# One stored row per node for both of its experts, and two groups of rows in the buffer, in a graph layer followed by a mixture of experts

## The chip, the cores and the metric

The kernel runs on one NeuronCore of a Trainium2 chip. A core has five engines with a queue each, which run their instructions in order and wait for each other through semaphores: TensorE (PE in the profile; its weight loads are the row PEld), VectorE (DVE), ScalarE (ACT), GpSimd (POOL) and SyncE (SP). Transfers go through 16 DMA engines; SP and POOL issue nearly all of them here. The metric is device time in microseconds of one launch, median of several runs. Every launch computes the whole reference, in float32.

## The reference

There are 6250 nodes with 256 features and 100,000 edges with 96 features, sorted by the node that they point to. The first half is a graph layer, the second half a mixture of 16 experts, of which each node uses two:

```python
out1 = segment_sum(edge_attr, col);  out2 = segment_max(edge_attr, col)
out3 = out1 / max(count, 1)
h = concat([layernorm(x), out1, out2, out3, u[batch]], axis=1)
x = x + relu(h @ W1 + b1) @ W2 + b2 + layernorm(x)

n = layernorm(x)
vals, idx = top_k(n @ gate_w + gate_b, 2)
wts = softmax(vals)
moe = sum(wts[k] * (relu(n @ w1[idx[k]] + b1[idx[k]]) @ w2[idx[k]] + b2[idx[k]]) for k in 0, 1)
x = x + layernorm(n + moe) * gamma + beta
```

## The kernel before

**Nodes.** Nodes are cut into 50 columns of 125 and these into 13 groups, the first of two columns and the others of four, taken from the last node to the first. A list of tasks with slot numbers (12 slots for a group) is sorted by slot, and within a slot by the order of entry; each task then appends its instructions to the engines' queues. A slot has no time: it only says where in the queues an instruction stands. The scan over the edges (`steps`, lines 298 to 302, on VectorE) is woven in between by a credit of estimated costs, so that it runs up to about 790 us.

**A group's way.** For a group that starts at slot B, the hidden layer (line 747) and the output layer (line 755) of the graph layer take the slots from B on. Its edge sums are gathered from memory by GpSimd (`take_edges`, line 698, and `take_carry`, line 705) and joined on VectorE (line 711). From slot B + 13 on, the group is prepared for the experts: `norm_b` (line 783, ScalarE) normalises the rows into the buffer `xr`; `turn_b` (line 792) transposes them on TensorE; `logits`, `choose`, `rank`, `rank_2` and `place` find the two best experts of each node, the two weights, and the place of the row in the list of each of the two experts; `send` (line 860) writes the rows to `xg_d` in memory, by two indirect transfers of GpSimd for each column, one for each expert.

**The row.** A row of `xg_d` is 256 normalised features, one weight and one number that says where the result is to go (`DR` = 258 words). The two copies of a node differ in those two words, so `xr` holds both: `[P, GS, 2, DR]`, in a pool with one buffer. `norm_b` of the next group therefore waits until all transfers of the group before have read the buffer.

**Experts.** `table_full` and `table_rest` cut the expert lists into 57 blocks of 256 rows. `to_row` turns a table of expert numbers and offsets into a row, from which SP reads registers in `load_block`: the block's rows `xb`, 1 MB of expert weights `wt` and a bias `eb`. `run_block(b)` runs two layers on TensorE (lines 1034 and 1047). Between the two halves of the first layer it calls `turn_block(b + 1)`, so on VectorE the order within a block is: the copy of the next block's transposed rows (line 1014), the bias added to its rows (line 1017), the destination (line 1019, or lines 1022 and 1023 from block 14 on), and only then the two activations of this block's second half (line 1038). The second layer needs four hidden parts of 128: parts 0 and 2 come from ScalarE (line 1040), parts 1 and 3 from line 1038, and TensorE takes them in the order 0, 2, 1, 3. After line 1050, ScalarE multiplies the rows by their weight (line 1052) and GpSimd scatters them to `y_d` (line 1053).

**End.** A last loop adds the two results of each node, normalises, and writes the output (lines 1365 to 1389).

Of the kernel before, what the change touches and what calls it, by code (L numbers as in the profile page):

```python
# [9 lines left out]
F32 = mybir.dt.float32  # L10
# [4 lines left out]
OP = mybir.AluOpType  # L15
# [4 lines left out]
P = 125  # L20
# [21 lines left out]
def kernel(  # L42
# [34 lines left out]
    B1O = W2O + FC * D  # L77
    WROW = B1O + FC
    NB = (2 * N - NE) // SB + NE
    DR = D + 2  # L80
    NG = (NT + GS - 1) // GS
    ER = EP * sum(JR)

# [16 lines left out]
    def halves(o, i):  # L100
# [14 lines left out]
    nc.gpsimd.memset(ones, 1.0)  # L115
    node_i = const.tile([P, NT], F32, name="node_i")
    nc.gpsimd.iota(node_i, pattern=[[P, NT]], base=0, channel_multiplier=1,
                   allow_small_or_imprecise_dtypes=True)
    place_i = const.tile([P, NT, 2], F32, name="place_i")
    nc.gpsimd.iota(place_i, pattern=[[P, NT], [N, 2]], base=0, channel_multiplier=1,  # L120
                   allow_small_or_imprecise_dtypes=True)
    erow = const.tile([P, NE], F32, name="erow")
    nc.gpsimd.iota(erow, pattern=[[N, NE]], base=0, channel_multiplier=0, allow_small_or_imprecise_dtypes=True)
# [64 lines left out]
    gtp = mlp.enter_context(tc.tile_pool(name="gt", bufs=2))  # L188
    sm = mlp.enter_context(tc.tile_pool(name="sm", bufs=2))
    xrp = mlp.enter_context(tc.tile_pool(name="xr", bufs=1))  # L190
    pTp = banks.enter_context(tc.tile_pool(name="pT", bufs=1, space=PSUM))
    accp = banks.enter_context(tc.tile_pool(name="acc", bufs=5, space=PSUM))
    pGp = banks.enter_context(tc.tile_pool(name="pG", bufs=1, space=PSUM))
# [583 lines left out]

    def norm_b(g):
        a, z = GRP[g]
        G[g]["xr"] = xr = xrp.tile([P, GS, 2, DR], F32, name="xr")  # L780
        for i in range(z - a):
            t = a + i
            nc.scalar.activation(xr[:, i, :, 0:D], G[g]["xt"][:, i, None, :].to_broadcast([P, 2, D]), AF.Identity,
                                 scale=stat[:, 0, t:t + 1], bias=stat[:, 1, t:t + 1])

    def turn_b(g, k):
        n = GRP[g][1] - GRP[g][0]
        if k == 0:
            G[g]["gT"] = gtp.tile([128, DC, GS * P], F32, name="gT", bufs=1)
        pT = pTp.tile([128, GS * P], F32, name="pT")  # L790
        for i in range(n):
            nc.tensor.transpose(pT[:, i * P:(i + 1) * P], G[g]["xr"][:, i, 0, k * 128:(k + 1) * 128], ident[:P, :P])
        nc.scalar.copy(G[g]["gT"][:, k, :n * P], pT[:, :n * P])

    def logits(g):
# [20 lines left out]
    def rank(g):  # L816
        a, z = GRP[g]
        n, m0 = z - a, NT - z
        i2 = gtp.tile([P, GS, 2], F32, name="i2")
        nc.vector.tensor_copy(i2[:, :n], G[g]["I8"][:, :n, 0:2])  # L820
        G[g]["mk"] = mk = gtp.tile([P, GS, 2, NE], F32, name="mk")
        nc.vector.tensor_tensor(mk[:, :n], i2[:, :n, :, None].to_broadcast([P, n, 2, NE]),
                                row_i[:P, None, None, 0:NE].to_broadcast([P, n, 2, NE]), op=OP.is_equal)
        mm = gtp.tile([P, GS, NE], F32, name="mm")
        nc.vector.tensor_add(mm[:, :n], mk[:, :n, 0], mk[:, :n, 1])
        for i in range(n):
            nc.vector.tensor_add(M[:, m0 + i + 1, :], M[:, m0 + i, :], mm[:, i, :])
        G[g]["mm"] = mm
# [9 lines left out]
    def place(g):  # L838
        a, z = GRP[g]
        n, xr, mk, dv = z - a, G[g]["xr"], G[g]["mk"], G[g]["dv"]  # L840

        rk = gtp.tile([P, GS, NE], F32, name="rk")
        nc.vector.tensor_tensor(rk[:, :n], G[g]["pR"][:, :n * NE].rearrange("p (i e) -> p i e", e=NE),
                                erow[:, None, :].to_broadcast([P, n, NE]), op=OP.add)
        nc.vector.tensor_tensor(mk[:, :n], mk[:, :n], rk[:, :n, None, :].to_broadcast([P, n, 2, NE]), op=OP.mult)
        posf = gtp.tile([P, GS, 2], F32, name="posf")
        nc.vector.tensor_reduce(posf[:, :n], mk[:, :n], AX.X, OP.add)
        G[g]["pos"] = pos = xrp.tile([P, GS, 2], I32, name="pos_i", bufs=2)
        nc.vector.tensor_copy(pos[:, :n], posf[:, :n])

        w0 = gtp.tile([P, GS], F32, name="w0")
        nc.vector.tensor_scalar(w0[:, :n], dv[:, :n], 1.0, None, op0=OP.add)
        nc.vector.reciprocal(w0[:, :n], w0[:, :n])
        nc.vector.tensor_copy(xr[:, :n, 0, D], w0[:, :n])
        nc.vector.tensor_mul(xr[:, :n, 1, D], w0[:, :n], dv[:, :n])
        nc.vector.tensor_copy(xr[:, :n, :, D + 1], place_i[:, a:z, :])  # L856

    def send(g, i):
        for k in range(2):
            d = nc.gpsimd.indirect_dma_start(out=xg_d[:, :],  # L860
                                             out_offset=IndirectOffsetOnAxis(ap=G[g]["pos"][:, i, k:k + 1], axis=0),
                                             in_=G[g]["xr"][:, i, k, :], in_offset=None)
            tc.declare_no_dep(d.ins, group="rows", reason="each row has a place of its own")
            tc.add_to_no_dep_group("rows", d.ins)
            nc.gpsimd.memset(gap, 0.0)
# [6 lines left out]
    def open_experts():  # L872
        edges_until(len(JR) - 1)
        assert next(stream, None) is None
        edges.close()
        MB["pools"] = pools = ExitStack()
        for nm, bufs in (("tb", 1), ("wp", 3), ("xg", 4), ("bk", 3)):
            MB[nm] = pools.enter_context(tc.tile_pool(name=nm, bufs=bufs, side="right"))
        tb = MB["tb"]
        MB["half"] = half = tb.tile([128, 2], F32, name="half_i")  # L880
        nc.gpsimd.iota(half, pattern=[[1, 2]], base=0, channel_multiplier=2, allow_small_or_imprecise_dtypes=True)
        MB["tab_a"] = tb.tile([1, 2, NA], I32, name="tab_a")
        MB["tab"] = tb.tile([1, 2, NB - NA], I32, name="tab")
        MB["seen"] = tb.tile([128, NB - NA], F32, name="seen")
        MB["more"] = tb.tile([1, 1], I32, name="more")
        for nm in ("cnt_e", "full", "nbf", "cum", "ge", "own"):
            MB[nm] = tb.tile([NB, NE], F32, name=nm)
        MB["nbi"] = tb.tile([NB, NE], I32, name="nbi")
        for nm in ("jc", "q", "skip"):
            MB[nm] = tb.tile([NB, 1], F32, name=nm)  # L890
        MB["er"] = tb.tile([NB, 2], F32, name="er")
# [33 lines left out]
        nc.vector.tensor_scalar(jc[:n], jc[:n], float(SB), None, op0=OP.mult)  # L925
        nc.vector.scalar_tensor_tensor(er[:n, 1:2], er[:n, 0:1], float(N), jc[:n], op0=OP.mult, op1=OP.add)

    def to_row(tab, n):
        pe = eps.tile([1, 2, n], F32, name="ps")
        for k in range(2):  # L930
            nc.tensor.matmul(pe[:, k, :], MB["er"][:n, k:k + 1], ident[:n, :n], start=True, stop=True)
        nc.vector.tensor_copy(tab, pe)

    def table_full_2():
        to_row(MB["tab_a"], NA)

    def table_rest():
        n = NB - NA
# [26 lines left out]

    def table_rest_2():
        n = NB - NA
        to_row(MB["tab"], n)
        ps = pGp.tile([128, n], F32, name="pg")
        nc.tensor.matmul(ps, MB["skip"][:n].to_broadcast([n, 128]), ident[:n, :n], start=True, stop=True)  # L970
        nc.vector.tensor_copy(MB["seen"], ps)
# [35 lines left out]
    def turn_block(b):  # L1007
# [7 lines left out]
        BL[b]["to"] = to_i = MB["xg"].tile([128, 2], I32, name="to_i")  # L1015

        nc.vector.tensor_tensor(xb[:, :, 0:D], xb[:, :, 0:D], BL[b]["eb"][:, None, :].to_broadcast([128, 2, D]), op=OP.add)
        if b < NA:
            nc.vector.tensor_copy(to_i, xb[:, :, D + 1])
        else:  # L1020
            far = MB["xg"].tile([128, 2], F32, name="far")
            nc.vector.tensor_scalar(far, MB["half"], MB["seen"][:, b - NA:b - NA + 1], float(2 * N), op0=OP.is_lt, op1=OP.mult)
            nc.vector.tensor_tensor(to_i, xb[:, :, D + 1], far, op=OP.add)

    def run_block(b, end):
        xT, wt, xb = (BL[b][nm] for nm in ("xT", "wt", "xb"))
# [22 lines left out]
        yb = MB["bk"].tile([128, 2, D], F32, name="yb")  # L1049
        nc.vector.tensor_tensor(yb, pY, xb[:, :, 0:D], op=OP.add)  # L1050
        for h in range(2):
            nc.scalar.activation(yb[:, h, :], yb[:, h, :], AF.Copy, scale=xb[:, h, D:D + 1])  # L1052
            d = nc.gpsimd.indirect_dma_start(out=y_d[:, :],  # L1053
                                             out_offset=IndirectOffsetOnAxis(ap=BL[b]["to"][:, h:h + 1], axis=0),
                                             in_=yb[:, h, :], in_offset=None, bounds_check=2 * N - 1, oob_is_err=False)
            tc.declare_no_dep(d.ins, group="back", reason="each row has a place of its own")
            tc.add_to_no_dep_group("back", d.ins)
            nc.gpsimd.memset(gap, 0.0)
# [29 lines left out]
    for g, (a, z) in enumerate(GRP):  # L1088
# [40 lines left out]
        at_slot(B + SLOTS + 9, rank_2, g)  # L1129
        at_slot(B + SLOTS + 10, place, g, cost=1.5)  # L1130
        for i in range(n):
            at_slot(B + SLOTS + 11 + i // 2, send, g, i)
    T = SLOTS * (NG - 3) + 21
    at_slot(T, open_experts)
    at_slot(T, count_full)
# [28 lines left out]

    def fill_rows():

        nc.vector.memset(fill[:, D + 1:], float(2 * N))
        for h in range(SB // 128):
            nc.gpsimd.dma_start(xg_d.rearrange("(e n) d -> n e d", n=N)[h * 128:(h + 1) * 128],
                                fill[:, None, :].to_broadcast([128, NE, DR]))  # L1170
# [37 lines left out]
    cut_x = windows_of(xrp.tile([P, GS, 2, DR], F32, name="xr"), 1)[0]  # L1208
# [229 lines left out]
```

## Time and profile before

| what | us |
|---|---|
| median of three runs | 1454.03 (1452.14 to 1459.58) |
| the profiled execution, its own time | 1462.48 |
| its span, first to last instruction | 1460.7 |
| TensorE busy (matmuls) | 1148.5 |
| VectorE busy | 915.6 |
| GpSimd busy | 527.8 |
| ScalarE busy | 511.0 |

In the profile, a row of a timeline gives the start in us, the duration, the engine, the line of the kernel, the operation, the tiles written and read with their shapes, and in brackets the idle time of the engine just before, with what ended it. A line of the waits gives the engine and its line, what it waited for, the total in us, the number of waits and the longest. A line of the windows gives the stretch, its length, then for each engine the busy time with the number of instructions, then the granted TensorE clock, the busy share of the DMA engines and GB/s.

The span has three parts. Up to about 905 us the graph layer and the routing run. From there to 1355 us the 57 expert blocks run, the first ten of them between the last pieces of the routing. The rest is the last loop.

### The profile page before, as it was taken

The numbers are of one execution on the slowest core, as the hardware profiler recorded it, in microseconds if no ns is written. First come the engines' busy times: TensorE is split into PE (matmuls) and PEld (weight loads), VectorE is DVE, ScalarE is ACT, GpSimd is POOL, SyncE is SP. The second block draws the span as 40 slices with busy tenths as digits, with TensorE's granted clock in tenths as the row PEclk, the third lists the DMA queues.
The fourth block names the chain that finished last, engine by engine and source line by source line (L and its number), as shares of the span: only waits on it lengthen the run. The fifth ranks groups of instructions, "written<-read, shape, count | busy, mean of one in ns | idle before, by whom it ended". The sixth has DMA issues, their size and how long they took to land.

```text
span 1460.7 us, 16116 instructions
## 1 busy us (share of the span) xinstructions
PE 1148.5 (79%) x4667; PEld 810.4 (55%) x4667; DVE 915.6 (63%) x2322; ACT 511.0 (35%) x1174; POOL 527.8 (36%) x611
## 2 busy tenths in 40 slices
PE   2857258978786879999688999899999999999200
PEld 1743144635443445655445567787888888888100
DVE  4487569959685979988688323244344544444397
ACT  3384125543445542542325441321212222212133
POOL 4133033563546553364242522234333333333100
PEclk9988579989988889999899999899999999999655
DMA  6726777787778897888887332646777787765695
GB/s 180 168 63 172 187 193 201 194 224 182 216 192 247 223 277 190 254 223 213 249 221 206 84 122 69 209 147 235 229 250 262 234 267 234 237 226 184 128 263 148
DMA packets 173812, 292.25 MB, mean 200 GB/s; under 512 B 30883, under 2 KB 119656, under 8 KB 166414
## 3 DMA queue, kind: packets, MB, share of 16 engines
q1 hardware_dynamic: 137374, 234.35, 56.0%
q0 software_dynamic: 36224, 56.33, 13.7%
q8 instruction: 40, 0.66, 0.2%
q14 instruction: 62, 0.51, 0.1%
q10 hardware_dynamic: 112, 0.41, 0.1%
HBM read 169.70 MB, written 123.21 MB: 201 GB/s over the span
## 4 chain that ended last, share of the span: by engine, by line
issue 27%; DVE 23%; DMA 18%; POOL 13%; PE 12%; ACT 3%; SPq 2%; POOLq 0%; DVEq 0%; ACTq 0%
POOL y_d L1053 9%; PE acc L747 5%; DMA raw<-in_edge_dram 5%; DMA cg<-carry_d,next_i 4%; DMA rows_d<-rw 3%; PE acc L755 3%; DVE rw L302 2%; DVE rw L299 2%; DVE rw L298 2%; DMA xg_d<-xr,pos_i 2%; DVE rw L301 2%; POOL gb L474 1%; PE acc L570 1%; DMA carry_d<-ct 1%; DVE o L1387 1%
## 5 line engine op out<-in xcount | busy, mean ns | idle before, releaser
L747 PE MATMUL acc<-inT,w1x 128*128 128x500 f32 (+1 forms) x832 | 375.9, 603 | 0.0
L747 PEld LDWEIGHTS acc<-inT,w1x 128*128 128x128 f32 x832 | 163.1, 204 | 179.1 <-issue 177.3
L1053 POOL DMA_INDIRECT y_d<-yb,to_i x114 | 134.5, 1180 | 295.6 <-ACT yb L1052 273.4
L1034 PE MATMUL acc<-xT,wt 128*128 128x256 f32 x912 | 225.6, 391 | 7.8 <-ACT hb L1040 6.2
L1047 PE MATMUL acc<-wt,hb 128*128 128x256 f32 x912 | 209.6, 383 | 3.6 <-DVE hb L1038 3.6
L860 POOL DMA_INDIRECT xg_d<-xr,pos_i x100 | 130.1, 1301 | 213.8 <-DVE xr L856 152.2
L755 PE MATMUL acc<-w2s,hT 128*125 128x256 f32 x800 | 193.5, 400 | 13.4 <-ACT hT L749 13.4
L1034 PEld LDWEIGHTS acc<-xT,wt 128*128 128x128 f32 x912 | 171.0, 193 | 40.2 <-ACT hb L1040 14.9
L1047 PEld LDWEIGHTS acc<-wt,hb 128*128 128x128 f32 x912 | 175.3, 192 | 29.0 <-DVE hb L1038 4.5
L755 PEld LDWEIGHTS acc<-w2s,hT 128*125 128x125 f32 x800 | 157.8, 201 | 39.5 <-ACT hT L749 14.2
L1052 ACT ACTIVATE yb<-yb,xb 128x256 f32<-128x256 f32 x114 | 51.8, 501 | 349.0 <-issue 291.6
L1050 DVE TENSOR_TENSOR yb<-acc,xb 128x512 f32<-128x512 f32 x57 | 39.4, 692 | 167.3 <-PE acc L1047 167.3
L749 ACT ACTIVATE hT<-acc,c 128x500 f32<-128x500 f32 (+1 forms) x104 | 68.5, 658 | 209.0 <-PE acc L747 209.0
L474 POOL DMA_INDIRECT gb<-in_dst_dram,blk_i x50 | 71.1, 1421 | 130.5 <-DVE blk_i L471 73.8
L301 DVE TENSOR_TENSOR rw<-rw,raw 125x768 f32<-125x768 f32 x88 | 83.6, 950 | 32.7 <-DMA raw<-in_edge_dram 32.7
L298 DVE TENSOR_TENSOR rw<-rw,keep 125x768 f32<-125x768 f32 x81 | 78.3, 966 | 34.0 <-DMA rows_d<-rw 23.7
L1014 DVE COPY xT<-pT 128x512 f32<-128x512 f32 x57 | 39.4, 690 | 72.4 <-PE pT L1012 71.5
L302 DVE TENSOR_TENSOR rw<-rw,raw 125x768 f32<-125x768 f32 x88 | 83.6, 950 | 0.0
L299 DVE TENSOR_TENSOR rw<-rw,bar 125x768 f32<-125x768 f32 x81 | 79.4, 981 | 0.0
L705 POOL DMA_INDIRECT cg<-carry_d,next_i x44 | 65.1, 1481 | 36.8 <-issue 23.6
L698 POOL DMA_INDIRECT at<-rows_d,first_i x44 | 60.0, 1363 | 37.2 <-PE acc L747 10.0
L732 ACT COPY inT<-pT 128x500 f32<-128x500 f32 (+1 forms) x65 | 36.0, 553 | 98.8 <-PE pT L731 94.8
(296 smaller groups left out, 1445.1 us busy)
## 6 DMA issues: line engine op xcount, KB each, us to landing
wt<-in_wpack_dram SPq DMA_DIRECT2D x57, 1026.0 KB
rows_d<-rw SPq DMA_DIRECT2D x27, 1440.0 KB
rows_d<-rw SPq DMA_DIRECT2D x27, 810.0 KB
raw<-in_edge_dram SPq DMA_DIRECT2D x27, 720.0 KB
xb<-xg_d SPq DMA_DIRECT2D x57, 258.0 KB
raw<-in_edge_dram SPq DMA_DIRECT2D x27, 405.0 KB
yk<-y_d SPq DMA_DIRECT2D x20, 400.0 KB
eb<-in_eb_dram SPq DMA_DIRECT2D x57, 128.0 KB
```

Source lines behind the costliest of these rows:

```text
L298: nc.vector.tensor_tensor(su, prev[0], keep[c][:, :, s + j, None].to_broadcast(bcast), op=OP.mult)
L299: nc.vector.tensor_tensor(mx, prev[1], bar[c][:, :, s + j, None].to_broadcast(bcast), op=OP.min)
L301: nc.vector.tensor_tensor(su, su, x_j, op=OP.add)
L302: nc.vector.tensor_tensor(mx, mx, x_j, op=OP.max)
L474: nc.gpsimd.indirect_dma_start(out=gbs_[t], out_offset=None, in_=dst_b, in_offset=IndirectOffsetOnAxis(ap=blk_i[:, t:t + 1], axis=0))
L747: nc.tensor.matmul(pH[:, :n * P], w1x[:, k, ms], inT[:, k, :n * P], start=False, stop=(k == KC - 1))
L749: nc.scalar.activation(h[:, :n * P], pH[:, :n * P], AF.Relu, bias=c1[:, m:m + 1])
L755: nc.tensor.matmul(pO, G[g]["hT"][m][:, i * P:(i + 1) * P], w2s[:, m, :], start=(m == 0), stop=(m == HC - 1))
L860: d = nc.gpsimd.indirect_dma_start(out=xg_d[:, :], out_offset=IndirectOffsetOnAxis(ap=G[g]["pos"][:, i, k:k + 1], axis=0), in_=G[g]["xr"][ ...
L1034: nc.tensor.matmul(pB[i][:, half, :], wt[:, k * FF + m * 128:k * FF + (m + 1) * 128], xT[:, k, :], start=(k == 0), stop=(k == DC - 1))
L1047: nc.tensor.matmul(pY[:, h, :], hb[:, m, h * 128:(h + 1) * 128], wt[:, W2O + m * D:W2O + (m + 1) * D], start=(m == order[0]), stop=(m == o ...
L1053: d = nc.gpsimd.indirect_dma_start(out=y_d[:, :], out_offset=IndirectOffsetOnAxis(ap=BL[b]["to"][:, h:h + 1], axis=0), in_=yb[:, h, :], in ...
```

## The change

Both transfers of a node now read one and the same row, which holds 256 features and four more words (`DR` = 260): the difference of the two weights, the second weight, the number of the first expert, and the destination for the second expert (the node's number plus `N`). `norm_b` writes 256 elements of a row in place of 512. `xr` is one tile `xr2` for two groups, and group `g` uses the half `g % 2`. The block finds out which of its rows are of their first expert: `to_row` also spreads the blocks' expert numbers over all partitions (`MB["of"]`), and `turn_block` compares, selects the weight and shifts the destination. The sends of all groups but the last four get slot numbers that are two higher. `place_i`, a table of both destinations, is gone.

```diff
-    DR = D + 2
+    DR = D + 4
...
-    place_i = const.tile([P, NT, 2], F32, name="place_i")
-    nc.gpsimd.iota(place_i, ...)
...
+    xr2 = xrp.tile([P, 2, GS, DR], F32, name="xr")
...
     def norm_b(g):
-        G[g]["xr"] = xr = xrp.tile([P, GS, 2, DR], F32, name="xr")
+        G[g]["xr"] = xr = xr2[:, g % 2]
...
-            nc.scalar.activation(xr[:, i, :, 0:D], G[g]["xt"][:, i, None, :].to_broadcast([P, 2, D]), AF.Identity,
+            nc.scalar.activation(xr[:, i, 0:D], G[g]["xt"][:, i, :], AF.Identity,
...
     def place(g):
...
-        nc.vector.tensor_copy(xr[:, :n, 0, D], w0[:, :n])
-        nc.vector.tensor_mul(xr[:, :n, 1, D], w0[:, :n], dv[:, :n])
-        nc.vector.tensor_copy(xr[:, :n, :, D + 1], place_i[:, a:z, :])
+        nc.vector.tensor_mul(xr[:, :n, D + 1], w0[:, :n], dv[:, :n])
+        nc.vector.tensor_sub(xr[:, :n, D], w0[:, :n], xr[:, :n, D + 1])
+        nc.vector.tensor_copy(xr[:, :n, D + 2], G[g]["i2"][:, :n, 0])
+        nc.vector.tensor_scalar(xr[:, :n, D + 3], node_i[:, a:z], float(N), None, op0=OP.add)
...
     def send(g, i):
...
-                                             in_=G[g]["xr"][:, i, k, :], in_offset=None)
+                                             in_=G[g]["xr"][:, i, :], in_offset=None)
...
+    def to_row(tab, n, b0):
+        ps = pGp.tile([128, n], F32, name="pg")
+        nc.tensor.matmul(ps, MB["er"][:n, 0:1].to_broadcast([n, 128]), ident[:n, :n], start=True, stop=True)
+        nc.vector.tensor_copy(MB["of"][:, b0:b0 + n], ps)
...
     def turn_block(b):
...
-        if b < NA:
-            nc.vector.tensor_copy(to_i, xb[:, :, D + 1])
-        else:
+        c1st, w = (MB["xg"].tile([128, 2], F32, name=nm) for nm in ("c1st", "w"))
+        BL[b]["w"] = w
+        nc.vector.tensor_scalar(c1st, xb[:, :, D + 2], MB["of"][:, b:b + 1], None, op0=OP.is_equal)
+        nc.vector.tensor_mul(w, c1st, xb[:, :, D])
+        nc.vector.tensor_add(w, w, xb[:, :, D + 1])
+        to = to_i if b < NA else MB["xg"].tile([128, 2], F32, name="to")
+        nc.vector.scalar_tensor_tensor(to, c1st, float(-N), xb[:, :, D + 3], op0=OP.mult, op1=OP.add)
+        if b >= NA:
             far = ...
             nc.vector.tensor_scalar(far, MB["half"], MB["seen"][:, b - NA:b - NA + 1], float(2 * N), ...)
-            nc.vector.tensor_tensor(to_i, xb[:, :, D + 1], far, op=OP.add)
+            nc.vector.tensor_tensor(to_i, to, far, op=OP.add)
...
-            nc.scalar.activation(yb[:, h, :], yb[:, h, :], AF.Copy, scale=xb[:, h, D:D + 1])
+            nc.scalar.activation(yb[:, h, :], yb[:, h, :], AF.Copy, scale=BL[b]["w"][:, h:h + 1])
...
-            at_slot(B + SLOTS + 11 + i // 2, send, g, i)
+            at_slot(B + SLOTS + (13 if g < NG - 4 else 11) + i // 2, send, g, i)
...
-        nc.vector.memset(fill[:, D + 1:], float(2 * N))
+        nc.vector.memset(fill[:, D + 3:], float(3 * N))
```

More of the change, by code (lines that the diff above doesn't have):

```diff
@@ L117 @@
     nc.gpsimd.iota(node_i, pattern=[[P, NT]], base=0, channel_multiplier=1,
-                   allow_small_or_imprecise_dtypes=True)
-    place_i = const.tile([P, NT, 2], F32, name="place_i")
-    nc.gpsimd.iota(place_i, pattern=[[P, NT], [N, 2]], base=0, channel_multiplier=1,
                    allow_small_or_imprecise_dtypes=True)
@@ L791, in turn_b @@
         for i in range(n):
-            nc.tensor.transpose(pT[:, i * P:(i + 1) * P], G[g]["xr"][:, i, 0, k * 128:(k + 1) * 128], ident[:P, :P])
+            nc.tensor.transpose(pT[:, i * P:(i + 1) * P], G[g]["xr"][:, i, k * 128:(k + 1) * 128], ident[:P, :P])
         nc.scalar.copy(G[g]["gT"][:, k, :n * P], pT[:, :n * P])
@@ L818, in rank @@
         n, m0 = z - a, NT - z
-        i2 = gtp.tile([P, GS, 2], F32, name="i2")
+        G[g]["i2"] = i2 = gtp.tile([P, GS, 2], F32, name="i2")
         nc.vector.tensor_copy(i2[:, :n], G[g]["I8"][:, :n, 0:2])
@@ L884, in open_experts @@
         MB["seen"] = tb.tile([128, NB - NA], F32, name="seen")
+        MB["of"] = tb.tile([128, NB], F32, name="of")
         MB["more"] = tb.tile([1, 1], I32, name="more")
@@ L926, in table_full @@
         nc.vector.scalar_tensor_tensor(er[:n, 1:2], er[:n, 0:1], float(N), jc[:n], op0=OP.mult, op1=OP.add)
-    def to_row(tab, n):
+    def to_row(tab, n, b0):
+        ps = pGp.tile([128, n], F32, name="pg")
+        nc.tensor.matmul(ps, MB["er"][:n, 0:1].to_broadcast([n, 128]), ident[:n, :n], start=True, stop=True)
+        nc.vector.tensor_copy(MB["of"][:, b0:b0 + n], ps)
         pe = eps.tile([1, 2, n], F32, name="ps")
@@ L934, in table_full_2 @@
     def table_full_2():
-        to_row(MB["tab_a"], NA)
+        to_row(MB["tab_a"], NA, 0)
     def table_rest():
@@ L967, in table_rest_2 @@
         n = NB - NA
-        to_row(MB["tab"], n)
+        to_row(MB["tab"], n, NA)
         ps = pGp.tile([128, n], F32, name="pg")
@@ L1207 @@
     w1u = wk.tile([P, GS, D], F32, name="xn", bufs=1).rearrange("p i d -> p (i d)")[:GF, 0:HID]
-    cut_x = windows_of(xrp.tile([P, GS, 2, DR], F32, name="xr"), 1)[0]
+    cut_x = windows_of(xr2, 1)[0]
     cut_w = w2s[:P].rearrange("p k d -> p (k d)")[:, 0:WE * EF].rearrange("p (k f) -> p k f", f=EF)
```

## The prediction

> **What bounds the kernel now.** I read the busy slices first, then the stretches by window, then what VectorE waits for, then single rows.
>
> ```profile
> PE   2857258978786879999688999899999999999200
> DVE  4487569959685979988688323244344544444397
> ```
>
> The two halves have different limits: up to slice 21 (800 us) both engines are busy, afterwards TensorE alone. The windows make it sharp:
>
> ```profile
> 485.00:560.00 75.00, 58.55 (x210) 35.10 (x209) 63.56 (x147) 31.98 (x74) 39.05 (x34) 0.89 0.87 244
> 1100.00:1200.00 100.00, 100.00 (x476) 85.75 (x476) 46.91 (x95) 21.18 (x52) 33.70 (x52) 1.00 0.79 258
> ```
>
> In the expert blocks TensorE is busy 100 of 100 us at clock 1.00, with a block every 7.58 us (row of line 1014 at 1142.02, then at 1149.60). Anything that stops TensorE there is paid in full, once per block. In the first part (here 485 to 560 us) no engine is full. Who leads is told by what VectorE waits for between 200 and 797 us:
>
> ```profile
> DVE at L711 <- DMA cg<-carry_d,next_i: 33.8, 8, 11.6
> DVE rw L301 <- DMA raw<-in_edge_dram: 32.7, 9, 6.7
> DVE rw L298 <- DMA rows_d<-rw: 23.7, 6, 9.2
> DVE rw L298 <- issue: 10.3, 2, 6.2
> ```
>
> The two rows left out are 1.2 and 0.2 us. VectorE waits for transfers and practically never for TensorE or ScalarE, while TensorE waits for VectorE (28.2 us at line 834 in the same stretch). So VectorE with the edge transfers leads there, and TensorE follows with slack.
>
> **The blocks, where the change adds work.** These rows are one block, VectorE's part and the TensorE weight load that needs its result:
>
> ```profile
> 1149.60 0.69 DVE L1014 COPY xT<-pT 128x512 f32<-128x512 f32 x1 [1.47 <-PE pT L1012]
> 1150.21 0.68 DVE L1017 TENSOR_TENSOR xb<-xb,eb 128x512 f32<-128x512 f32 x1
> 1150.81 0.22 DVE L1022 TENSOR_SCALAR far<-half_i,seen 128x2 f32<-128x2 f32 x1
> 1151.07 0.16 DVE L1023 TENSOR_TENSOR to_i<-xb,far 128x2 int32<-128x2 f32 x1
> 1151.18 0.95 DVE L1038 TENSOR_SCALAR hb<-acc,wt 128x256 f32<-128x256 f32 x2
> ...
> 1152.01 0.19 PEld L1047 LDWEIGHTS acc<-wt,hb 128*128 128x128 f32 x1
> ```
>
> Line 1038 makes hidden parts 1 and 3; by its single rows they end at 1151.66 and 1152.12. TensorE loads part 1 at 1152.01 and part 3 at 1152.45. So the results are 0.35 and 0.32 us early. How early they must be is shown where TensorE really waited for line 1038, near 996 us:
>
> ```profile
> 995.70 0.86 DVE L1038 TENSOR_SCALAR hb<-acc,wt 128x256 f32<-128x256 f32 x2
> 996.22 0.19 PEld L1047 LDWEIGHTS acc<-wt,hb 128*128 128x128 f32 x1 [2.28 <-DVE hb L1038]
> ```
>
> The first of that pair ended at 996.17, the load began 0.05 later. The true cover is 0.30 us for part 1 and 0.27 for part 3; part 3 follows part 1 at once on VectorE and decides.
>
> The change puts four small operations in front of line 1038 (from block 14 on): compare, multiply, add, and the scaled shift of the destination; lines 1022 and 1023 stay. Steps from start to start, from the rows: an operation with a pointer scalar until one that needs its result, 0.26 (1150.81 to 1151.07); a small two-input operation until one that needs it, 0.16 + 0.04 = 0.20; until one that does not, 0.08 to 0.11 (1151.07 to 1151.18). The new chain is compare 0.26, multiply 0.20, add 0.09, shift 0.09, far 0.26, destination 0.11: 1.01. The old one is 0.26 + 0.11 = 0.37. Line 1038 comes 0.64 later; with 0.08 for the free steps 0.62, which I take. Ends: all four steps free, 4 x 0.09 = 0.36; all at 0.26, 1.04. TensorE then stops 0.62 - 0.27 = 0.35 us per block (0.09 to 0.77). It concerns `turn_block` of blocks 14 to 56, 43 times: **+15 us** (4 to 33). Nothing takes it back: the copy in line 1014 waits for TensorE's transposes (1.47 us idle), so the whole round moves.
>
> [...] But the row of line 1023 has 0.16 us for two elements[...]. The row decides; a chain of such operations costs its waits too.
>
> Blocks below 14: three operations more, old step 0.11, new 0.26 + 0.20 + 0.08 + 0.11 = 0.65, so 0.54 later. Where TensorE's own matmul holds part 3 (ends 0.71 to 0.77 apart), this fits; four early blocks whose parts end 0.53 apart lose about 0.2 each. At 996 and 1008 us VectorE is already late and 0.54 comes straight through, but the second wait (for a bias that lands at 1006.9) absorbs the first, so 0.5 once. Together +1.3. `to_row`'s new matmul and copy stand before that same wait of 1.8 us and cost nothing; without that cover, some 0.7.
>
> ScalarE's scale now waits for `w`, made a block earlier: nothing. Rows of 1040 bytes for 1032: 0.8% of transfers of 258 KB a block, hidden as all block loads are.
>
> **The first part, where the change takes away.** `norm_b` no longer waits for the sends of the group before: in the built program its waits name them no more, only those two groups back. Before, ScalarE lost 57.2 us there in seven waits (26.6 + 20.3 + 6.7 + 3.6 by the transfer that landed last), and TensorE's transposes behind them 36 of their 42.3 us at line 792. Also 50 activations shrink from 0.80 us to about 0.50 (line 1052 has 256 elements at 501 ns): 15 us of an engine busy a third of the time.
>
> This is not 57 or 36 us of the span, because VectorE leads and waits for neither. It gains only where the late ScalarE held GpSimd, whose gather VectorE needs:
>
> ```profile
> 309.66 2.93 ACT L783 ACTIVATE xr<-xt,stat 125x512 f32<-125x512 f32 x4 [13.05 <-DMA gb<-in_dst_dram,blk_i]
> ...
> 315.33 1.21 POOL L474 DMA_INDIRECT gb<-in_dst_dram,blk_i  x1 [4.10 <-ACT junk L481]
> ...
> 327.26 0.94 DVE L711 SCALAR_TENSOR_TENSOR at<-cg,cross,at 125x96 f32<-125x96 f32 x1 [10.19 <-DMA cg<-carry_d,next_i]
> ```
>
> Line 481 stands behind line 783 on ScalarE, line 474 waits for it, and the gather of `cg` is next on GpSimd. So 4.1 of VectorE's 10.2 us go. The same at 450.8 (4.7 us on GpSimd, VectorE's wait 3.2: gain 3.2) and 528.1 (6.3; wait 1.2: gain 1.2). Sum 8.5. At 584, 696 and 767 us the ScalarE waits (4.2, 3.6, 6.7) are followed by waits of VectorE for edge transfers alone, where I see no link. What is late next is those edge transfers: in 485 to 560 us the DMA engines are at 0.87, and an earlier VectorE may wait for them instead. I take 7 of 8.5; ends 0 and 16 (twice the sum, if GpSimd's wait of 12.5 us at 489 also goes, since TensorE's earlier stop delayed ScalarE there).
>
> Against it: `place` has one operation and one dependent step more, 0.2 us on VectorE for each of ten groups: +2. Net **-5** (-14 to +2).
>
> The sends' two slots do nothing. In the built programs the queues of GpSimd, SP and ScalarE hold the same operations in the same order (GpSimd's lacks `place_i`, 0.67 us at the start, when its next wait is 6.6 us). No GpSimd task lies in the slots passed; GpSimd still stands at the first send until `place` is done, with the gathers behind it. The padding value 3N costs nothing.
>
> **Sum**, on the profiled execution: span 1460.7 + 15 + 1.3 - 5 = 1472. Its own time, 1462.5, is 0.6% above the median; on the median 1454 + 11 = **1465 us**.
>
> **Rivals.**
> 1. The small operations overlap or fit. For: [...]VectorE is busy only 47 of 100 us there. Against: the measured steps. Blocks +2, first part -5: about 1452.
> 2. The blocks lose as said, but the first part gives nothing, VectorE waiting for edges in place of `cg`: 1454 + 16 + 2 = 1472.
> 3. The other side: TensorE's lost time in the first part comes through. Place: line 792 at 310, 446, 523 and 768 us (10.0 + 10.5 + 8.6 + 3.7 of the 36). For: the stops lie on the chain that ended last, and the clock is 0.5 after them. Against: TensorE meets VectorE again soon after (6.4 us idle at 403, 6.1 at 476, 11.3 at 732). If those 36 come, 1454 - 36 + 16 = 1434. It decides once more than 23 us of them reach 790 us.
> 4. Doing nothing: for the sends this is so; for `norm_b` the waits exclude it.
>
> **How the numbers follow.** Main case 0.54, rival 1 0.20, rival 2 0.16, rival 3 0.10. A measurement tells 0.5%, 7.3 us, from no change: slower means above 1461.3, faster below 1446.8. The main case's own range is 1457 to 1474 (first part -12 to +1, blocks +9 to +21), of which about four fifths is above 1461.3; rival 2 is slower; rival 1 is mostly same. Slower 0.43 + 0.15 + 0.02 = 0.60; faster 0.09 from rival 3 and 0.03 from rival 1: 0.12; same 0.28. The range goes from rival 1's 1451 to 1476 above rival 2.
>
> **What would show it.** A block every 7.93 us instead of 7.58; six small VectorE rows between the bias addition and the activations of `hb`; TensorE waiting about 0.35 us for `hb` before the second layer in 43 blocks; no wait of ScalarE at `norm_b`; the `cg` waits of VectorE down from 33.8 to about 25 us; the first block starting some 5 us earlier. I am wrong if the spacing stays below 7.7, or if the first block starts over 15 us earlier.

## The result and the profile after

| | before | after |
|---|---|---|
| median of 20 runs each | 1459.26 us (1452.14 to 1467.06) | 1468.14 us (1463.82 to 1477.06) |
| the profiled execution, its own time | 1462.48 us | 1467.32 us |
| span | 1460.7 us | 1465.5 us |

The ratio is 1.007, with a 95% interval of 1.0053 to 1.0088: the change makes the kernel about 10 us slower. The prediction said 1465 us, 11 above a median of 1454 from three runs; with 20 runs that median is 1459, and the step up is 9 to 10 us.

The busy slices of the profile after:

```profile
PE   2757268969695869799697999899999999999200
DVE  4487678979676979888678224454455555544397
```

In slices 26 to 37, the blocks, VectorE has gone from mostly 4 tenths to 4 and 5, and TensorE shows a 9 in all but one, as before. The window over a hundred microseconds of blocks (columns as before) shows what the digits hide:

```profile
1100.00:1200.00 100.00, 99.22 (x455) 80.52 (x455) 52.48 (x141) 20.08 (x50) 31.33 (x50) 1.00 0.74 241
```

455 matmuls in place of 476 in the same time, at the same clock: TensorE does 4% less. The busy time hides it: in this trace the stop shows as idle time of the weight load, and a matmul's end is modelled. One block, as rows of the timeline of the kernel after:

```profile
1145.34 0.69 DVE L1017 COPY xT<-pT 128x512 f32<-128x512 f32 x1 [1.47 <-PE pT L1015]
1145.94 0.68 DVE L1020 TENSOR_TENSOR xb<-xb,eb 128x512 f32<-128x512 f32 x1
1146.02 1.46 POOL L1062 DMA_INDIRECT y_d<-yb,to_i  x1 [0.23 <-issue]
1146.54 0.22 DVE L1024 TENSOR_SCALAR c1st<-xb,of 128x2 f32<-128x2 f32 x1
1146.80 0.16 DVE L1025 TENSOR_TENSOR w<-c1st,xb 128x2 f32<-128x2 f32 x1
1147.00 0.16 DVE L1026 TENSOR_TENSOR w<-w,xb 128x2 f32<-128x2 f32 x1
1147.07 0.15 DVE L1028 SCALAR_TENSOR_TENSOR to<-c1st,xb 128x2 f32<-128x2 f32 x1
1147.14 0.33 DVE L1031 TENSOR_SCALAR far<-half_i,seen 128x2 f32<-128x2 f32 x1
1147.51 0.16 DVE L1032 TENSOR_TENSOR to_i<-to,far 128x2 int32<-128x2 f32 x1
1147.62 0.88 DVE L1047 TENSOR_SCALAR hb<-acc,wt 128x256 f32<-128x256 f32 x2
1148.15 1.38 PEld L1056 LDWEIGHTS acc<-wt,hb 128*128 128x128 f32 x7 [0.43 <-DVE hb L1047]
```

The six small operations stand in front of `hb`, and the weight load waits 0.43 us for `hb`, which it did not before. The median spacing of blocks 13 to 55, by the starts of line 1017, is 7.880 us; before it was 7.580. Line `far` takes 0.33 us here and took 0.22 before; this becomes important below.

The first part, by what VectorE waits for between 200 and 797 us, what TensorE waits for in the same stretch, and the group of `norm_b`:

```profile
DVE rw L299 <- DMA raw<-in_edge_dram: 35.1, 11, 6.9
DVE rw L296 <- DMA rows_d<-rw: 27.7, 8, 8.8
DVE at L709 <- DMA cg<-carry_d,next_i: 25.9, 9, 12.1
...
PE pg L832 <- DVE mm L823: 61.0, 6, 14.0
```

```profile
L781 ACT ACTIVATE xr<-xt,stat 125x256 f32<-125x256 f32 x50 | 25.9, 588 | 1.4 <-DVE rsa L672 1.3
```

ScalarE's 57 us in front of `norm_b` are gone. TensorE did not get them: it waits 61.0 us for VectorE at line 832, where it waited 28.2. VectorE's waits for `cg` fell from 33.8 to 25.9, those for edge transfers rose from 56.4 to 62.8.

Where the two profiled executions differ, by the starts of the copy to `xT`:

| stretch | before | after | difference |
|---|---|---|---|
| start to block 0 | 903.5 | 901.0 | -2.5 |
| block 0 to 13 | 117.2 | 110.7 | -6.5 |
| block 13 to 55 | 318.4 | 331.1 | +12.7 |
| block 55 to the end | 121.6 | 122.7 | +1.1 |
| span | 1460.7 | 1465.5 | +4.8 |

The third row is the one that was forecast. The second was not, and the last experiment shows that it is mostly chance. The fourth lies within the 121.3 to 123.3 us that this stretch takes over the profiles of all runs below.

### The profile page after: what moved, and what is told of

It is laid out like the page before. It is cut to its first block, busy times and chain, and to the rows that moved or that the text cites. A ratio compares the mean times of both kernels' runs of the same rounds, so it can differ in the third digit from the quotient of the medians.

```text
span 1465.5 us, 16306 instructions
## 1 busy us (share of the span) xinstructions
PE 1143.2 (78%) x4671; PEld 800.1 (55%) x4671; DVE 949.3 (65%) x2551; ACT 500.6 (34%) x1174; POOL 535.5 (37%) x610
## 5 line engine op out<-in xcount | busy, mean ns | idle before, releaser
L745 PE MATMUL acc<-inT,w1x 128*128 128x500 f32 (+1 forms) x832 | 362.6, 586 | 0.0
L745 PEld LDWEIGHTS acc<-inT,w1x 128*128 128x128 f32 x832 | 157.7, 197 | 170.4 <-issue 168.5
L1043 PE MATMUL acc<-xT,wt 128*128 128x256 f32 x912 | 221.2, 385 | 7.3 <-ACT hb L1049 5.3
L1056 PE MATMUL acc<-wt,hb 128*128 128x256 f32 x912 | 220.6, 387 | 4.7 <-DVE hb L1047 3.2
L753 PE MATMUL acc<-w2s,hT 128*125 128x256 f32 x800 | 201.9, 413 | 16.0 <-ACT hT L747 16.0
L1056 PEld LDWEIGHTS acc<-wt,hb 128*128 128x128 f32 x912 | 167.9, 191 | 48.0 <-DVE hb L1047 24.5
L753 PEld LDWEIGHTS acc<-w2s,hT 128*125 128x125 f32 x800 | 163.7, 209 | 44.7 <-ACT hT L747 16.8
L1061 ACT ACTIVATE yb<-yb,w 128x256 f32<-128x256 f32 x114 | 51.7, 500 | 358.1 <-issue 311.3
L472 POOL DMA_INDIRECT gb<-in_dst_dram,blk_i x50 | 77.5, 1549 | 122.1 <-DVE blk_i L469 78.8
L296 DVE TENSOR_TENSOR rw<-rw,keep 125x768 f32<-125x768 f32 x81 | 81.8, 1009 | 35.1 <-DMA rows_d<-rw 27.7
```

The costliest lines, as they stand in the source:

```text
L296: nc.vector.tensor_tensor(su, prev[0], keep[c][:, :, s + j, None].to_broadcast(bcast), op=OP.mult)
L472: nc.gpsimd.indirect_dma_start(out=gbs_[t], out_offset=None, in_=dst_b, in_offset=IndirectOffsetOnAxis(ap=blk_i[:, t:t + 1], axis=0))
L745: nc.tensor.matmul(pH[:, :n * P], w1x[:, k, ms], inT[:, k, :n * P], start=False, stop=(k == KC - 1))
L753: nc.tensor.matmul(pO, G[g]["hT"][m][:, i * P:(i + 1) * P], w2s[:, m, :], start=(m == 0), stop=(m == HC - 1))
L1043: nc.tensor.matmul(pB[i][:, half, :], wt[:, k * FF + m * 128:k * FF + (m + 1) * 128], xT[:, k, :], start=(k == 0), stop=(k == DC - 1))
L1056: nc.tensor.matmul(pY[:, h, :], hb[:, m, h * 128:(h + 1) * 128], wt[:, W2O + m * D:W2O + (m + 1) * D], start=(m == order[0]), stop=(m == o ...
```

## The experiments

Ratios are to the kernel before, with 95% intervals. "Spacing" is the median over blocks 13 to 55. Four kernels were run once, for their profile (three operations, independent operations, strided operands, and the kernel before again); spacings, rows and stage times are read from those, not ratios.

### Is it the selection in front of hb?

The selection goes behind the two activations of `hb`, in front of `yb`, where VectorE idled (before the change it waited 167.3 us for TensorE there, in 57 waits at line 1050):

```diff
     def turn_block(b):
...
+    def pick_block(b):
+        xb, to_i = BL[b]["xb"], BL[b]["to"]
         c1st, w = (MB["xg"].tile([128, 2], F32, name=nm) for nm in ("c1st", "w"))
...
     def run_block(b, end):
...
+        if b + 1 < end:
+            pick_block(b + 1)
         pY = acc().rearrange("p (h d) -> p h d", h=2)
...
     at_slot(T, turn_block, 0)
+    at_slot(T, pick_block, 0)
```

> The changed kernel with the selection (compare, multiply, add, shift, far, destination) moved behind the two second-half activations of hb, in front of yb. Theory (the dependent small operations in front of hb cost the blocks 0.30 us each, 43 times): spacing of the blocks back from 7.88 to 7.58 us, TensorE's wait for hb near zero, total 13 us below the changed kernel, about 1455 us, ratio to the kernel before 0.997. Rival (the longer spacing comes from something else in the block, the longer rows or the spread expert numbers): spacing stays above 7.8, ratio 1.007. Rival (moved, the operations delay yb and the scatter instead): spacing 7.58 but a later last block, ratio between 1.000 and 1.005.

Measured: 1455.13 us (1448.47 to 1461.11), ratio 0.9962 (0.9942 to 0.9981), spacing 7.580. The rows of one block:

```profile
1144.96 0.68 DVE L1020 TENSOR_TENSOR xb<-xb,eb 128x512 f32<-128x512 f32 x1
1145.55 0.48 DVE L1049 TENSOR_SCALAR hb<-acc,wt 128x256 f32<-128x256 f32 x1
1145.90 2.35 PEld L1060 LDWEIGHTS acc<-wt,hb 128*128 128x128 f32 x11
1146.38 0.48 DVE L1049 TENSOR_SCALAR hb<-acc,wt 128x256 f32<-128x256 f32 x1 [0.35 <-PE acc L1045]
1146.79 0.22 DVE L1026 TENSOR_SCALAR c1st<-xb,of 128x2 f32<-128x2 f32 x1
```

`hb` now waits for TensorE, not the reverse. Blocks 13 to 55 take 318.4 us, as before the change. This version beats both kernels.

The counterpart puts the cost into the kernel before and nothing else of the change:

```diff
...
+        nc.vector.tensor_scalar(c1, xb[:, :, D + 1], ident[:, 0:1], None, op0=OP.is_equal)
+        nc.vector.tensor_mul(w1, c1, xb[:, :, D])
+        nc.vector.tensor_add(w1, w1, xb[:, :, D + 1])
+        nc.vector.scalar_tensor_tensor(w3, c1, float(-N), xb[:, :, D + 1], op0=OP.mult, op1=OP.add)
         if b < NA:
```

> The kernel before plus four small operations in turn_block in front of hb, chained as in the change (compare with a pointer scalar, multiply, add, scaled shift) with results that nobody uses; all else as before. Theory: spacing 7.88 us as in the changed kernel, 42 x 0.30 = 13 us more, ratio 1.009. The stretch of blocks 0 to 13 stays near 121.6 us plus 1. Rival (the small operations fit under the cover): spacing 7.6, ratio 1.000 to 1.002. If part of the 0.30 comes from the wider rows: spacing 7.7 to 7.8.

Measured: 1472.65 us, ratio 1.0105 (1.0074 to 1.0135), spacing 7.882, blocks 13 to 55 in 330.7 us. The four operations give the whole block loss by themselves; the longer rows and the spread expert numbers have no part in it. Both runs came out as expected, but for one figure: the 121.6 us named there for blocks 0 to 13 are those of the stretch behind block 55, which took 122.8 us here; blocks 0 to 13 took 112.4.

### What in the selection costs it?

The same insertion with three of the four operations (no shift):

> The kernel before plus three of the four small operations (compare, multiply, add; no scaled shift); their results are not used. In the run with four, line far took 0.33 us instead of 0.22 and hb came 0.71 later. From its steps, three are 0.071 shorter. Theory A (cover of 0.41 us, reckoned to the matmul and not to the weight load; far at its 0.22): hb 0.53 us later, spacing 7.58 + 0.12 = 7.70 us. Theory B (far stays at 0.33): hb 0.64 later, spacing 7.81. Theory C (far ends when GpSimd's scatter instruction ends, wherever it starts): far 0.40, hb 0.71 later, spacing 7.88 as with four. With the cover of 0.27 that the prediction took, A would give 7.84.

Measured: spacing 7.884. One operation less costs the same. Rows of a block (VectorE and GpSimd):

```profile
1137.88 1.06 POOL L1057 DMA_INDIRECT y_d<-yb,to_i  x1 [0.23 <-issue]
1138.00 0.22 DVE L1019 TENSOR_SCALAR c<-xb,ident 128x2 f32<-128x2 f32 x1
1138.26 0.16 DVE L1020 TENSOR_TENSOR w<-c,xb 128x2 f32<-128x2 f32 x1
1138.46 0.16 DVE L1021 TENSOR_TENSOR w<-w,xb 128x2 f32<-128x2 f32 x1
1138.53 0.40 DVE L1026 TENSOR_SCALAR far<-half_i,seen 128x2 f32<-128x2 f32 x1
1138.97 0.16 DVE L1027 TENSOR_TENSOR to_i<-xb,far 128x2 int32<-128x2 f32 x1
```

`far` starts earlier and takes longer: it ends at 1138.93 or 1138.94, and GpSimd's scatter ends at 1138.94. Over the blocks of the kernel after, of the run with four operations and of this one, the scatter's end lies 4 to 8 ns behind that of `far` every time, though `far` starts 0.34 us before it in the first two and 0.41 us in this one. Theory C holds: the fourth operation runs in time that `far` waits anyway. The scatter does not wait for `far`: its median length is 1.46 us in the kernel before, where `far` isn't held, and the same in these three (in ten of the 43 blocks it is 1.06, as in these rows, and the end of `far` follows it there too).

The same four kinds of operations, none needing another's result:

```diff
...
+        nc.vector.tensor_mul(w1, xb[:, :, D + 1], xb[:, :, D])
+        nc.vector.tensor_add(w2, xb[:, :, D], xb[:, :, D + 1])
+        nc.vector.scalar_tensor_tensor(w3, xb[:, :, D], float(-N), xb[:, :, D + 1], op0=OP.mult, op1=OP.add)
```

> The kernel before plus four small operations of the same kinds, none of which needs another's result; results not used. Theory (a dependent step costs the operation's whole latency, a free one 0.07 to 0.11 us): about 0.35 us instead of 0.60 for the four, under the cover of 0.41: spacing 7.58 to 7.62. If the count of operations decides and not the dependence: spacing 7.88. If far is held until GpSimd's scatter instruction ends: 7.88 too, but then far itself takes 0.5 us or more.

Measured: spacing 7.580. The rows:

```profile
1139.93 1.47 POOL L1058 DMA_INDIRECT y_d<-yb,to_i  x1 [0.23 <-issue]
1140.46 0.22 DVE L1019 TENSOR_SCALAR c<-xb,ident 128x2 f32<-128x2 f32 x1
1140.59 0.16 DVE L1020 TENSOR_TENSOR w<-xb 128x2 f32<-128x2 f32 x1
1140.66 0.16 DVE L1021 TENSOR_TENSOR w<-xb 128x2 f32<-128x2 f32 x1
1140.73 0.16 DVE L1022 SCALAR_TENSOR_TENSOR w<-xb 128x2 f32<-128x2 f32 x1
1140.80 0.23 DVE L1027 TENSOR_SCALAR far<-half_i,seen 128x2 f32<-128x2 f32 x1
1141.06 0.16 DVE L1028 TENSOR_TENSOR to_i<-xb,far 128x2 int32<-128x2 f32 x1
```

The steps from start to start are 0.13, 0.07, 0.07 and 0.07 us, where the dependent ones were 0.26, 0.20, 0.08 and 0.07. `hb` comes 0.35 us later than before the change, and the blocks do not notice. `far` starts 0.59 us before the scatter's end and is not held. The operation behind it, `to_i`, starts 0.34 us before that end, where `far` was held in the kernel after, and takes its 0.16 us. (The run's total of 1468.02 us comes from elsewhere: its first part took 4 us more than that of before, blocks 0 to 13 took 118.1 us with 17 us at half clock, and blocks 13 to 55 took 318.7.)

What holds `far`? I tried its operands, as strided ones:

```diff
-        MB["half"] = half = tb.tile([128, 2], F32, name="half_i")
+        MB["half"] = half = tb.tile([128, 2, 2], F32, name="half_i")[:, :, 0]
-            far = MB["xg"].tile([128, 2], F32, name="far")
+            far = MB["xg"].tile([128, 2, 2], F32, name="far")[:, :, 0]
```

> The changed kernel with every second word of the tiles half and far used, so that the two elements of line far lie 8 bytes apart; nothing else moves. In three arrangements far ended where GpSimd's scatter instruction ends, 0.11 to 0.18 us late. Theory (a dense float32 operation from SBUF to SBUF[...] is held until GpSimd's instruction ends, a strided one is not): far 0.22 us, hb 0.60 later than before instead of 0.71, spacing 7.58 + 0.60 - 0.41 = 7.77 us. Rival (held whatever its operands, or by something else): far 0.33, spacing 7.88.

Measured: spacing 7.883, `far` 0.329 us. My theory, that operands lying close together make the difference, falls. That `far` ends with the scatter is shown, and so is that operations of other forms were not held: in the run with independent operations `to_i` with its two inputs ran freely at the same moment (0.34 us before the scatter's end), and so did `hb`, which reads PSUM (started 0.22 us before the scatter's end, it took its usual 0.48 us). Which property of `far` it is, and why it was held when it started 0.34 or 0.41 us before the scatter's end and not at 0.59, stays open. The scatter itself was not moved, so a third event at the same moment, which holds only such operations, isn't excluded either.

The practical test is to reorder the selection of the changed kernel so that each operation has another between itself and the one it needs, and `far` is early:

```diff
         nc.vector.tensor_scalar(c1st, ...)
+        nc.vector.tensor_scalar(far, ...)
         nc.vector.tensor_mul(w, c1st, xb[:, :, D])
-        nc.vector.tensor_add(w, w, xb[:, :, D + 1])
...
         nc.vector.scalar_tensor_tensor(to, c1st, ...)
-        nc.vector.tensor_scalar(far, ...)
+        nc.vector.tensor_add(w, w, xb[:, :, D + 1])
         nc.vector.tensor_tensor(to_i, to, far, op=OP.add)
```

> The changed kernel with the same six small operations in another order: compare, far, multiply, shift, add, destination, so that no one directly follows the one it needs, and far starts before the time at which it was held. Theory: far 0.22, hb 0.25 to 0.35 us later than before, under the cover of 0.41: spacing 7.58, total as with the late selection, about 1455, ratio 0.996 to 0.997. If the count of operations decides: spacing 7.8 or more and 1467.

Measured: 1453.79 us, ratio 0.9971 (0.9955 to 0.9988), spacing 7.580, `hb` 0.33 us later than before, `far` 0.22 us. The rows:

```profile
1141.48 0.22 DVE L1024 TENSOR_SCALAR c1st<-xb,of 128x2 f32<-128x2 f32 x1
1141.61 0.22 DVE L1027 TENSOR_SCALAR far<-half_i,seen 128x2 f32<-128x2 f32 x1
1142.18 0.88 DVE L1048 TENSOR_SCALAR hb<-acc,wt 128x256 f32<-128x256 f32 x2
```

Six operations in front of `hb` fit, if they stand in the right order. This order ends two things at once, the dependent steps and the hold of `far`; no run has dependent steps without the hold.

### What does the first part give?

The sends at their old slot (`11` for all groups):

> The changed kernel with the sends of all groups at the slot of before (11). Theory (the order on every queue is the same, the two slots do nothing): the time of the changed kernel, 1468, ratio to the kernel before 1.007, first block at 904 us. If the slots matter, the first block moves by several us either way and the ratio leaves 1.005 to 1.009.

Measured: 1468.06 us, ratio 1.006 (1.0036 to 1.0084), first block at 898.6 us, not the expected 904, and 2.4 us earlier than in the profile after. By the total the slots do nothing; what the first block moved is within what equal first parts show below.

One half of the buffer for all groups, first in the changed kernel, then in the version with the late selection:

```diff
-        G[g]["xr"] = xr = xr2[:, g % 2]
+        G[g]["xr"] = xr = xr2[:, 0]
```

> The changed kernel with all groups using half 0 of the row buffer, so that norm_b waits again for the sends of the group before. Theory (VectorE leads in the first part, the wait is worth only what late gathers cost it): first block 3 to 6 us later than in the changed kernel, total about 1472, ratio to the kernel before 1.010; ScalarE's waits at norm_b near 57 us again, VectorE's waits for cg near 34. Rival (the first part gives nothing): 1468, ratio 1.006 to 1.007. Rival (TensorE's lost time in the first part counts in full): 1468 + 36 = 1504, ratio 1.03.

> The kernel with the late selection, with all groups on half 0 of the row buffer. Theory (two halves are what the first part gains): first block near 903 us instead of 899, total 4 us above the late selection with both halves, about 1459, ratio to the kernel before 0.999 to 1.000; spacing 7.58. Rival (the halves give nothing, the late selection gains by something else): 1455, ratio 0.996. Rival (TensorE's lost time counts in full): 1455 + 36.

Measured: 1470.75 us, ratio 1.0062 (1.0039 to 1.0085), and 1453.35 us, ratio 0.9962 (0.9946 to 0.9978). By the ratios neither is slower than its partner with two halves (1.007 and 0.9962); the first block came at 903.1 and 895.6 us, 2.1 later and 3.2 earlier than the partner's, where 3 to 6 later was expected. But ScalarE waited only 40.2 and 38.6 us at `norm_b`, in 18 and 15 waits, where it had waited 57.2 in seven before the change: by these counts half a tile comes free column by column, and a tile taken anew from a pool as a whole. So this wasn't the old wait. Two more runs, on the late selection, bring that back: the buffer from a pool of one; and the same with activations of 512 elements, as before.

```diff
-        G[g]["xr"] = xr = xr2[:, g % 2]
+        G[g]["xr"] = xr = xrp.tile([P, 2, GS, DR], F32, name="xr")[:, 0]
...
```

and in the second run also

```diff
...
-            nc.scalar.activation(xr[:, i, 0:D], G[g]["xt"][:, i, :], AF.Identity,
+            nc.scalar.activation(xr[:, :, i, 0:D], G[g]["xt"][:, i, None, :].to_broadcast([P, 2, D]), AF.Identity,
...
```

> The late selection with the row buffer taken anew from a pool of one buffer for each group, as in the kernel before, so that norm_b waits until all sends of the group before are done (with half 0 of one tile it waited only column by column, 40 us); norm_b still writes 256 elements. Theory of the prediction (the wait holds GpSimd's gathers, cg waits 35 us again): 4 to 6 us above the late selection, ratio 0.999 to 1.000, first block near 903 us. Rival (the wait is worth nothing, VectorE waits for edges instead): 1454 to 1456, ratio 0.996.

> As the run before it in this list, and norm_b writes 512 elements in each activation again (the second 256 go to a half that nobody reads): the first part's ScalarE work and wait are those of the kernel before. If the wait and the width together are the gain of the first part: ratio 1.000. If the width alone gives the gain: 1.000 here and 0.996 in the run with 256. If neither matters and the gain lies elsewhere (the sends, place, or the blocks): 0.996 here too.

Measured: 1454.81 us, ratio 0.9975 (0.9958 to 0.9991) with 256 elements, and 1459.79 us, ratio 1.001 (0.9995 to 1.0024) with 512. The groups of `norm_b`, first with 256, then with 512 elements, and VectorE's wait for `cg` in the former:

```profile
L780 ACT ACTIVATE xr<-xt,stat 125x256 f32<-125x256 f32 x50 | 25.9, 588 | 53.5 <-DMA gb<-in_dst_dram,blk_i 27.6 <-DMA at<-rows_d,first_i 12.8 <-DMA xg_d<-xr,pos_i 8.4
```

```profile
L781 ACT ACTIVATE xr<-xt,stat 125x512 f32<-125x512 f32 x50 | 36.6, 801 | 49.8 <-DMA at<-rows_d,first_i 26.2 <-DMA xg_d<-xr,pos_i 18.3 <-DMA carry_d<-ct 5.4
```

```profile
DVE at L708 <- DMA cg<-carry_d,next_i: 34.7, 9, 11.8
```

With the wait back (53.5 us) and the `cg` waits back (34.7 us; 22.2 in the late selection with two halves), the kernel is at 0.9975 against 0.9962: 1.9 us, which the intervals cannot tell from nothing (nor from some 5). With the width back as well, the whole gain is gone: 5.0 us between the two medians, and the intervals don't overlap, though the `cg` waits are no higher (33.8 us). So where the wait is in place, the width of the activations, 50 times 0.21 us, is worth about 5 us; and removing the wait from the narrow activations gains nothing that these runs show. The fourth combination, two halves with activations of 512 elements, was not run: that the two halves alone would have gained the 5 us too, each change being enough by itself, is not excluded.

Of the 5 us the profiles place 0.86: from block 3 to 4 stand 10.17 us with 256 elements and 11.03 with 512 wherever the clock was full, which is the four activations of the last group between the blocks (4 x 0.21). Where the rest comes out isn't shown: the first block starts at 901.2 us with 256 and at 901.0 with 512.

### Why were blocks 0 to 13 faster?

> The kernel before once more, unchanged, for its clock. Theory (the 6.5 us that blocks 0 to 13 took less in the profile after are windows of half clock, which differ from run to run): few or none of them between 915 and 1000 us, blocks 0 to 13 in 110 to 113 us instead of 117.2, span about 1455. Rival (the windows belong to the kernel before): 117 us again, with half clock at 925 and 946 us.

Measured: 1456.32 us, span 1454.5, blocks 0 to 13 in 114.6 us. Two windows in the profile before, then in this one, then in the one after (the last three columns are clock, share of the DMA engines, GB/s):

```profile
920.00:940.00 20.00, 17.24 (x71) 14.19 (x70) 6.44 (x14) 6.55 (x13) 4.20 (x8) 0.83 0.52 181
940.00:960.00 20.00, 17.62 (x80) 15.06 (x78) 5.65 (x23) 4.35 (x8) 3.16 (x6) 0.83 0.38 124
```

```profile
920.00:940.00 20.00, 15.61 (x80) 13.62 (x81) 6.18 (x12) 6.47 (x14) 5.59 (x11) 0.97 0.61 213
940.00:960.00 20.00, 18.51 (x80) 15.89 (x80) 8.01 (x32) 4.08 (x8) 2.23 (x6) 0.86 0.35 129
```

```profile
920.00:940.00 20.00, 16.42 (x91) 13.86 (x89) 7.04 (x18) 6.35 (x15) 6.23 (x11) 1.00 0.63 220
940.00:960.00 20.00, 18.51 (x93) 15.68 (x93) 10.05 (x40) 5.81 (x12) 3.50 (x9) 1.00 0.47 160
```

The low stretches stand at 0.50 (before, from 925.3 to 932.0 and from 945.7 to 952.5 us). A clock of 0.83 over 20 us is then 6.8 us at half clock, so up to 3.4 us lost in each of the two windows of before, 6.8 together; after has none there. Over blocks 0 to 13 the half clock takes 17 us before, 10 in the second profile of the same program, and 3.4 after. Among the profiles of all experiments the stage runs from 109.1 us (no half clock) to 118.1 (17 us of it), in kernels of both kinds. My theory was half right: the windows come and go, but 114.6 is above the 110 to 113 that I expected. In this stage they were 6.8, 6.8 and 3.4 us long before, and one of 3.4 us after. The 6.5 us are not a gain of the change, except for the 0.86 above.

## Why the prediction was right, and where its steps were not

**The bound and the mechanism: right.** (The slice up to which both engines are busy is the 22nd, which ends at 803 us.) TensorE sets the pace of the blocks, and the selection in front of `hb` stops it. The two counterparts show it from both sides: 318.4 us without the operations in front, 330.7 with them alone.

**The size, 0.35 us a block, 15 us in all: measured 0.300 and 12.7 to 13, by two terms that were both mis-sized.** `hb` came 0.71 us later, not 0.62. Five of the six steps measured as forecast (compare 0.26, multiply 0.20, add 0.08, shift 0.07, destination 0.11); `far` was forecast at 0.26 and took 0.37, held until the scatter's end, which no row of before could show, as `far` stood earlier there (it started 0.94 us before that end and took its 0.22). Against that, the cover was not 0.27 but 0.41. The step that failed was reading it at the weight load, and at part 3: in the medians over the blocks the load that needs part 1 comes 0.41 us late, but the load and the matmul behind it only 0.30, and so it stays. By these figures that load starts 0.11 us before it must, and this lead has to be added to the 0.30 us of part 1. Part 1 decides and not part 3, whose load comes 0.37 us late but its matmul 0.30, like the one before. With both terms right, 0.71 - 0.41 = 0.30. Without the hold it would be, as an estimate from the same figures, 0.60 - 0.41 = 0.19, some 8 us of 13.

**"Free steps" and dependent steps: right, and decisive.** The prediction put a free step at 0.08 to 0.11 and a dependent one at 0.20 to 0.26. The run with independent operations pays nothing, the one with dependent ones 13 us, the hold of `far` included. Four independent operations moved `hb` by 0.35 us, which is still under the cover of 0.41. Rival 1 (they overlap or fit) is wrong for the order as written and right for the reordered one.

**Blocks below 14, +1.3: not resolved.** The two runs with added operations and one half-clock window took 112.4 and 112.2 us, the changed kernel with one 110.7, the late selection with none 109.1; the clock moves more than the term.

**The first part, -5: the size fits, the reason isn't borne out.** The wait at `norm_b` went and the `cg` waits fell by 7.9 of the forecast 8.5. In that profile VectorE's waits for edge transfers rose, as the prediction feared (56.4 to 62.8 us), but in the late selection, whose first part is the same, they did not (53.5). The step that failed is the path from the `cg` waits to the end: bringing the wait back raises them by 12.5 us and costs 1.9 us that the runs cannot tell from nothing. What shows is what the prediction put at nothing, the shorter activations ("15 us of an engine busy a third of the time"): about 5 us with the wait in place, of which 0.86 lies between the blocks. They took 0.59 us, not 0.50. So rival 2 may be right about the wait, and then the forecast sum came out by another term, which is luck; whether two halves with the long activations would have gained as much stays open. The first block started 2.5 us earlier instead of 5; over the profiles it began between 898.4 and 907.5 us with the first part of before and between 898.1 and 901.1 with that of after, so one pair cannot tell 5 from nothing.

**Rival 3, TensorE's 36 us: excluded.** TensorE's lost time moved into line 832 (28.2 to 61.0 us), and the first block came 2.5 us earlier, far from 36.

**The sends' slots, nothing: right.** **The 3N, `to_row`, the longer rows: nothing seen**; the inserted four operations alone give the loss, and the version with late selection, old wait and old width, which keeps all of these, stands at 1.001.

**The sum.** +13 from the blocks and -5 for the first part leave +8, and 9 to 10 were measured. The prediction's 11 was close because its errors were small and of both signs, not because each step stood.

## What to carry to other kernels

On an engine in order, ask not only how many operations a change adds in front of an awaited one but how many of them depend on the one just before (0.20 and 0.26 us a step here, against 0.07 and 0.13): reordering, or moving them behind the awaited result, turned a kernel 0.7% slower into one 0.3 to 0.4% faster. Read the slack of a result at the matmul that stalls and not at its weight load, which ran 0.11 us ahead here. Before a stage's difference between two profiles is explained, compare its granted clock and take a second profile of the same program.

## What the runs showed of the hardware

- In the blocks a small VectorE operation with a pointer scalar (`far`, 0.22 us alone) took 0.33 and 0.40 us when it started 0.34 and 0.41 us before the end of a GpSimd indirect transfer's instruction, and ended 4 to 8 ns before that end; started 0.59 us before it, it took 0.22. An operation with two inputs that started 0.34 us before that end kept its 0.16 us, and one that reads PSUM, 0.22 us before it, its 0.48. When this hold sets in, and by what, these runs do not show.
- Two small VectorE operations started 0.07 to 0.08 us apart when the second did not need the first, though each took 0.15 to 0.16 us, and 0.20 when it did; after one with a pointer scalar it was 0.13 and 0.26 (the rows of the kernel after and of the run with independent operations).
- With the row buffer taken anew from a pool for each group, ScalarE waited 53.5 us at `norm_b`, in seven waits (the run with 256 elements); with one half of a tile that stays, 40.2 and 38.6 us, in 18 and 15 waits.
